# Attention scores of sixteen small heads: sixteen tiles of 32 by 32 of the array in place of four of 32 by 128

## The chip, the core and the metric

The kernel runs on one core of a Trainium2 chip. A core has five engines that run at the same time and wait for one another through semaphores: TensorE (PE, matrix products), VectorE (DVE), ScalarE (ACT), GpSimd (POOL) and SyncE (SP, which here only issues DMAs). PE reads both operands from SBUF and writes its results to PSUM. A PE product takes two kinds of instruction: a weight load puts the stationary operand into the array (the profile calls this row PEld), and a matmul then streams the moving operand through it (row PE). All data here are f32, and one product of the program becomes two weight loads and two matmuls in the profile; this text calls such a load and matmul together a pass, so a product has two passes. (A transpose through PE has one.)

The metric is device time in microseconds (us) of one execution. Lower is better.

## The reference

Sixteen independent sequences of 256 positions with 256 channels go through two blocks. Every attention has 16 heads of 16 channels.

- Block 0: adaptive layer norm from `cond`; self-attention in windows of 128 positions (shifted by 64); adaptive layer norm; cross-attention to a context of 256 positions that keeps only the 16 largest scores of each row; adaptive layer norm; a gated feed-forward with 1024 hidden channels. Each part is added to the residual through a gate.
- Block 1: adaptive layer norm of the sequence and of the context, full cross-attention of 256 queries to 256 keys, projection, residual.

Cut to the lines that the change touches, the scores are

```python
scores = jnp.einsum('bnqhd,bnkhd->bnhqk', q, k) / jnp.sqrt(jnp.float32(D))   # block 0, windows of 128
scores = jnp.einsum('bqhd,bkhd->bhqk', q, k) / jnp.sqrt(jnp.float32(D))      # block 0, top 16 of 256 keys
top_s, top_i = jax.lax.top_k(scores, TOPK)
scores = jnp.einsum('bqhd,bkhd->bhqk', q, k) / jnp.sqrt(jnp.float32(dh))     # block 1, 256 keys
```

with D = dh = 16: every score is a sum over only 16 products.

## The kernel before, in words

The whole program is unrolled: 16 sequences, one after another, overlapped like a pipeline. The helpers record operations (`op`) with an engine, a cost, the buffers that they read and write and a due time from a table (`DUE`, written out by hand for every operation). `Plan.order` sorts all operations by due time; each engine then executes its own operations in exactly that order. Nothing is reordered at run time between operations of one engine, so an operation that waits holds up everything behind it on its engine. Costs and due times only shape the order when the program is built.

PSUM has eight banks, each 128 partitions by 512 f32 values (buffers `W`). A score operation takes four of them at once.

How the scores are laid out: queries and keys are channel-major, 128 channels (8 heads) in the partitions. A strip of 32 partitions holds two heads of 16 channels; the keys `k2` exist twice, each copy with the other head's channels replaced (`by_parity`), so a product over 32 partitions gives the scores of one head. The helper `four` (L681) records one PE operation that does the four strips of 32 partitions: strip j uses rows 32j to 32j+31 of the array and writes its own bank j. Such a product uses 32 rows and 128 columns of the array; the four strips lie in different rows, so that they can run at the same time. This text calls one such operation a score group. There are five kinds, named by their line before the change:

- L948, `topk_round`: 128 queries against 256 keys for two heads: one product of 512 columns in each strip.
- L1067, `last_attention`, first half: scores of which only the row maxima are taken (`maxima`, DVE): two products of 256 columns in each strip.
- L1079, `last_attention`, second half: the scores again, transposed (keys in the partitions), for the exponentials on ACT: two products of 256 columns in each strip (four of 128 in the last sequence, which is done in two tiles).
- L901, `self_attention`, first half, for the row maxima: four products of 128 columns in each strip.
- L909, `self_attention`, second half, transposed: four products of 128 columns in each strip (two in sequence 15).

Between the two halves, `lower` (L710) turns the row maxima on DVE (L716) and writes them with eight small DMAs on SP's queue for each half of the heads (L723) into unused rows of the queries `q2`, so that the second half's product subtracts them by itself. Each of these DMAs writes one block of 32 columns (`k` in its loop) in every group of 128 of `q2`. It has to wait until the first half's products have read what it overwrites, and the second half's products wait for it.

After the exponentials, `weighted` (L699) multiplies them with the values. It is a PE operation of another shape: 128 rows and 17 columns of the array, four products side by side in four different groups of 32 columns (`po.t[ds(NW * j, DH + 1), ...]`). Before a score group, and after it, PE usually does other products of 128 by 128.

The stationary operand of a score product, which is loaded as weights, is a block of 128 queries (L948, L1067, L901) or 128 keys (L1079, L909), `ts(k, P)` in the code; the moving operand is the other one.

## Time and profile before

| | us |
|---|---|
| median of 3 runs | 1333.25 (1332.62 to 1334.47) |
| the profiled execution | 1333.42 |
| its span, first to last instruction | 1331.6 |
| PE busy | 1317.7 (99%), 13476 matmuls and as many weight loads |
| DVE busy | 1201.9 (90%) |
| ACT busy | 1019.5 (77%) |
| POOL busy | 1019.4 (77%) |

The profiled execution took 1.8 us more than its span, for what lies before the first and after the last instruction. Matmuls are pipelined and their ends are modelled, so that PE's busy share says little by itself; the chain of work that ended last says more. In it, each piece is given with its start, the time until the next piece, the line and the number of instructions.

The instructions of the five score lines in the profile: 512 matmuls of L948, 1024 of L1067, 960 + 128 of L1079, 1024 of L901 and 1024 of L909, 4672 in all, each with a weight load of 128 columns.

### The profile page before, as it was taken

The numbers are of one execution on the slowest core, as the hardware profiler recorded it, in microseconds if no ns is written. First come the engines' busy times: TensorE is split into PE (matmuls) and PEld (weight loads), VectorE is DVE, ScalarE is ACT, GpSimd is POOL, SyncE is SP. The second block draws the span as 40 slices with busy tenths as digits, with TensorE's granted clock in tenths as the row PEclk, the third lists the DMA queues.
The fourth block names the chain that finished last, engine by engine and source line by source line (L and its number), as shares of the span: only waits on it lengthen the run. The fifth ranks groups of instructions, "written<-read, shape, count | busy, mean of one in ns | idle before, by whom it ended". The sixth has DMA issues, their size and how long they took to land.

```text
span 1331.6 us, 38422 instructions
## 1 busy us (share of the span) xinstructions
PE 1317.7 (99%) x13476; PEld 1029.3 (77%) x13476; DVE 1201.9 (90%) x4298; ACT 1019.5 (77%) x2359; POOL 1019.4 (77%) x1522
## 2 busy tenths in 40 slices
PE   8999999999999999999999999999999999999998
PEld 6778887777878787787878777787878777786885
DVE  5698988999999999999999999999999999999844
ACT  3698878778787777878777877868777786977774
POOL 3587886868878786887869687887978688878862
PEclk9999999999999999999999999999999999999999
DMA  5454122102011110201111110101111020100000
GB/s 182 156 194 169 43 81 66 50 10 65 3 27 50 33 50 19 57 8 36 35 26 50 26 50 10 49 19 27 49 26 50 12 57 2 48 20 11 16 2 18
DMA packets 71647, 63.31 MB, mean 48 GB/s; under 512 B 38595, under 2 KB 57583, under 8 KB 71199
## 3 DMA queue, kind: packets, MB, share of 16 engines
q1 hardware_dynamic: 71455, 60.86, 15.6%
q8 instruction: 107, 1.75, 0.5%
q14 instruction: 85, 0.70, 0.2%
HBM read 45.58 MB, written 14.73 MB: 45 GB/s over the span
## 4 chain that ended last, share of the span: by engine, by line
PE 83%; DVE 12%; POOL 1%; DMA 1%; SPq 1%; issue 1%; ACT 0%; POOLq 0%; DVEq 0%; ACTq 0%
PE W L1009 18%; PE W L594 10%; PE W L699 9%; PE W L1036 8%; PE W L644 7%; PE W L1079 6%; PE W L948 5%; PE W L677 5%; PE W L630 4%; DVE nm L706 3%; DVE rest L975 3%; PE W L909 3%; DVE top L967 2%; PE W L901 2%; PE W L568 2%; PE W L1067 2%
## 5 line engine op out<-in xcount | busy, mean ns | idle before, releaser
L996 POOL TENSOR_TENSOR prT<-rest,prT 128x512 f32<-128x512 f32 x256 | 324.2, 1274 | 101.5 <-DVE rest L992 97.2
L706 DVE TENSOR_REDUCE nm<-W 128x2 f32<-128x512 f32 (+1 forms) x384 | 238.0, 678 | 22.3 <-PE W L1067 15.1
L1009 PE MATMUL W<-xT,w_L_xcond_w_m 128*128 128x256 f32 (+1 forms) x1088 | 257.4, 374 | 0.2 <-ACT xT L582 0.2
L980 ACT ACTIVATE prT<-W,ntop 128x256 f32<-128x256 f32 x512 | 214.4, 501 | 43.8 <-POOL ntop L969 38.0
L730 ACT ACTIVATE pTO<-W 128x512 f32<-128x512 f32 (+1 forms) x392 | 205.4, 611 | 33.1 <-PE W L1079 27.8
L1009 PEld LDWEIGHTS W<-xT,w_L_xcond_w_m 128*128 128x128 f32 x1088 | 185.0, 190 | 53.6 <-ACT pTO L730 10.6
L975 DVE MATCH_REPLACE8 rest<-top,W 128x256 f32<-128x256 f32 x512 | 207.4, 415 | 0.0
L967 DVE MAX8 top<-W 128x8 f32<-128x256 f32 x512 | 184.9, 415 | 24.1 <-PE W L948 24.1
L992 DVE MATCH_REPLACE8 rest<-top,rest 128x256 f32<-128x256 f32 x512 | 204.8, 409 | 0.0
L987 DVE MAX8 top<-rest 128x8 f32<-128x256 f32 x512 | 186.8, 409 | 0.0
L647 ACT ACTIVATE pTT<-W 128x512 f32<-128x512 f32 x256 | 152.2, 617 | 2.8 <-PE W L644 2.5
L644 PE MATMUL W<-ident,prT 128*128 128x128 f32 x1024 | 140.2, 274 | 0.2 <-POOL prT L996 0.2
L644 PEld LDWEIGHTS W<-ident,prT 128*128 128x128 f32 x1024 | 120.4, 141 | 17.5 <-POOL prT L996 0.4
L1036 PE MATMUL W<-w_L_xcond_w_m,h 128*128 128x256 f32 x512 | 113.8, 380 | 0.0
L1026 POOL TENSOR_TENSOR mb<-ma,mb 128x256 f32<-128x256 f32 (+1 forms) x136 | 95.1, 700 | 24.3 <-ACT mb L1024 21.6
L1036 PEld LDWEIGHTS W<-w_L_xcond_w_m,h 128*128 128x128 f32 x512 | 97.0, 190 | 14.5 <-POOL h L1029 1.1
L660 POOL TENSOR_TENSOR on<-tr,rec 128x256 f32<-128x256 f32 (+1 forms) x132 | 65.2, 503 | 49.4 <-DVE rec L659 49.3
L1029 POOL TENSOR_TENSOR h<-h,mb 128x256 f32<-128x256 f32 (+1 forms) x136 | 94.8, 697 | 8.7
L699 PE MATMUL W<-pTO,v 128*17 128x128 f32 (+1 forms) x2112 | 99.2, 323 | 0.0
L657 DVE STREAM_TRANSPOSE tr<-W 128x512 f32<-128x512 f32 (+1 forms) x132 | 72.6, 552 | 27.0 <-PE W L699 17.0
L1024 ACT ACTIVATE mb<-W,half 128x256 f32<-128x256 f32 (+1 forms) x136 | 68.7, 506 | 34.8 <-PE W L1009 34.0
L1019 ACT ACTIVATE h<-W,half 128x256 f32<-128x256 f32 (+1 forms) x136 | 68.7, 505 | 24.3 <-PE W L1009 24.2
(129 smaller groups left out, 2653.9 us busy)
## 6 DMA issues: line engine op xcount, KB each, us to landing
gate<-gates SPq DMA_DIRECT2D x48, 256.0 KB
q<-nmT SPq DMA_DIRECT2D x480, 1.0 KB
kept_k<-k SPq DMA_DIRECT2D x13, 512.0 KB
k<-kept_k SPq DMA_DIRECT2D x13, 512.0 KB
cx<-in_ctx_dram SPq DMA_DIRECT2D x19, 256.0 KB
kept_v<-v SPq DMA_DIRECT2D x13, 272.0 KB
v<-kept_v SPq DMA_DIRECT2D x13, 272.0 KB
cx<-in_ctx_dram SPq DMA_DIRECT2D x104, 32.0 KB
```

What stands on the lines that cost most here:

```text
L644: nc.tensor.transpose(w.t[:, ts(n, P)], flat[:, ts(n, P)], ident)
L699: nc.tensor.matmul(po.t[ds(NW * j, DH + 1), ds(q0, nq)], v.t[:, kt, 8 * m + 2 * j + a, :], pT.t.rearrange("p n q -> p (n q)")[:, ds(part, ...
L706: op("DVE", 0.61, lambda j=j, s=s: nc.vector.tensor_reduce(nm.t[:, k, ds(j, groups, step=4)], s.t.rearrange("p (g k) -> p g k", g=groups), ...
L730: op("ACT", 0.24 + q * 0.0005, lambda s=s, pT=pT: nc.scalar.activation(pT.t.rearrange("p n q -> p (n q)")[:, :q], s.t[:, :q], AF.Exp), r=[ ...
L967: nc.vector.max(top.t[:, a, 0:8], s.t[:, ts(a, L)])
L975: nc.vector.match_replace(rest.t[:, a, :], top.t[:, a, 0:8], s.t[:, ts(a, L)], TAKEN)
L980: nc.scalar.activation(pr.t[:, a, :], s.t[:, ts(a, L)], AF.Exp, bias=ntop.t[:, a:a + 1])
L987: nc.vector.max(top.t[:, a, 8:16], rest.t[:, a, :])
L992: nc.vector.match_replace(rest.t[:, a, :], top.t[:, a, 8:16], rest.t[:, a, :], TAKEN)
L996: op("POOL", 1.25, lambda: nc.gpsimd.tensor_tensor(pr.t, rest.t, pr.t, ALU.mult), r=[rest, pr], w=[pr])
L1009: nc.tensor.matmul(w.t[:, :q], w_m1.t[:, c, ds(n0, P)], xT.t[:, c, :q], start=c == 0, stop=c == NCC - 1)
L1036: nc.tensor.matmul(pp.t[:, ts(k, C)], hs[f].t[:, ts(k, P)], w_m2.t[:, f, :], start=f == 0, stop=f == NHC - 1)
```

## The change

Every score product is cut into four: the stationary operand's 128 columns are loaded as four blocks of 32 (`NW` = 32), each with a product of its own that writes 32 of the bank's 128 partitions. So a product uses 32 rows and 32 columns of the array, and a score group addresses sixteen such tiles in place of four. The moving operand, the results, the banks, the costs given to the planner, the due times and with them the order of all operations stay as they are. Within a group, the loop goes over the pieces, then over the four column blocks `c`, then over the four strips `j`.

```diff
         def all_of_them():
             for piece in pieces:
-                for j, s in zip(groups, banks):
-                    emit(slice(32 * j, 32 * j + 32), s.t, *piece)
+                for c in range(P // NW):
+                    for j, s in zip(groups, banks):
+                        emit(slice(32 * j, 32 * j + 32), s.t[ts(c, NW)], NW * c, *piece)
...
-                            lambda rows, s, n, m, a, k=k: nc.tensor.matmul(
-                                s[:, ts(n, P)], q2.t[rows, m, a, ts(k, P)], k2.t[rows, m, a, ts(k, P)], start=True, stop=True),
+                            lambda rows, s, at, n, m, a, k=k: nc.tensor.matmul(
+                                s[:, ts(n, P)], q2.t[rows, m, a, ds(k * P + at, NW)], k2.t[rows, m, a, ts(k, P)], start=True, stop=True),
...
-        banks, made = four([()], lambda rows, s: nc.tensor.matmul(
-            s, q.t[rows, m, ts(k, P)], k2.t[rows, m, :, :], start=True, stop=True),
+        banks, made = four([()], lambda rows, s, at: nc.tensor.matmul(
+            s, q.t[rows, m, ds(k * P + at, NW)], k2.t[rows, m, :, :], start=True, stop=True),
```

The other three calls of `four` (L909, L1067 and L1079) change in the same way: the stationary operand's `ts(k, P)` or `ts(kt, P)` becomes a block of 32 columns that starts at `at`. One line is added ahead of these calls, so the lines after L686 are numbered one higher after the change.

In the built program the score products grow from 2336 to 9344. With two passes each, PE has 27492 matmuls and 27492 weight loads in place of 13476 of each. The other engines' work is the same, instruction for instruction, but the semaphore waits change: which block of `q2` each small DMA of `lower` has to wait for is now known by blocks of 32 columns, so that 529 waits of their own stand in front of these DMAs on SP in place of 155. DVE gets 109 more waits of their own (509 in place of 400), most of them in front of the maxima of the top-16 search (L967) and the row maxima (L706).

More of the change, by code (lines that the diff above doesn't have):

```diff
@@ L908, in self_attention @@
             banks, _ = four([(nt * a + k, a, k) for a in range(2) for k in range(nt)],
-                            lambda rows, s, n, a, k, m=m: nc.tensor.matmul(
-                                s[:, ts(n, P)], k2.t[rows, m, a, ts(k, P)], q2.t[rows, m, a, ts(k, P)], start=True, stop=True),
+                            lambda rows, s, at, n, a, k, m=m: nc.tensor.matmul(
+                                s[:, ts(n, P)], k2.t[rows, m, a, ds(k * P + at, NW)], q2.t[rows, m, a, ts(k, P)], start=True, stop=True),
                             0.45 * nt, [(q2, m), (k2, m)], pTs)
@@ L1066, in last_attention @@
             for k in range(nt):
-                banks, _ = four([(a,) for a in range(2)], lambda rows, s, a, k=k, m=m: nc.tensor.matmul(
-                    s[:, ts(a, L)], q2.t[rows, m, a, ts(k, P)], k2.t[rows, m, a, :], start=True, stop=True),
+                banks, _ = four([(a,) for a in range(2)], lambda rows, s, at, a, k=k, m=m: nc.tensor.matmul(
+                    s[:, ts(a, L)], q2.t[rows, m, a, ds(k * P + at, NW)], k2.t[rows, m, a, :], start=True, stop=True),
                     0.87, [(q2, m), (k2, m)], [nm])
@@ L1078, in last_attention @@
                 banks, _ = four([(NT * e + kt, a, kt) for e, a in enumerate(pair) for kt in range(NT)],
-                                lambda rows, s, n, a, kt, m=m: nc.tensor.matmul(
-                                    s[:, ts(n, q)], k2.t[rows, m, a, ts(kt, P)], q2.t[rows, m, a, :q], start=True, stop=True),
+                                lambda rows, s, at, n, a, kt, m=m: nc.tensor.matmul(
+                                    s[:, ts(n, q)], k2.t[rows, m, a, ds(kt * P + at, NW)], q2.t[rows, m, a, :q], start=True, stop=True),
                                 0.87, [(q2, m), (k2, m)], pTs)
```

## The prediction

> **What bounds the kernel now.** I read the page first: the busy shares, the granted clock, the chain that ended last; then PE's waits, then the chain in order of time, then single stretches of a few hundredths of a us.

> ```profile
> span 1331.6 us, 38422 instructions
> PE 1317.7 (99%) x13476; PEld 1029.3 (77%) x13476; DVE 1201.9 (90%) x4298; ACT 1019.5 (77%) x2359; POOL 1019.4 (77%) x1522
> PEclk9999999999999999999999999999999999999999
> PE 83%; DVE 12%; POOL 1%; DMA 1%; SPq 1%; issue 1%; ACT 0%; POOLq 0%; DVEq 0%; ACTq 0%
> ```

> PE is busy all the time, at the full granted clock, and it carries 83% of the chain. Its waits, longest first, add up to a few us:

> ```profile
> PE W L807 <- DVE h L802: 3.7, 1, 3.7
> PE W L594 <- ACT xT L582: 1.1, 2, 0.5
> PE W L781 <- DMA h<-in_L_xcond_b_ada_dram: 0.9, 1, 0.9
> PE W L677 <- DVE oT L667: 0.8, 3, 0.3
> PE W L909 <- DMA q<-nmT: 0.6, 1, 0.6
> ```

> So whatever a score group becomes longer or shorter by goes one to one into the time, as long as nothing else comes late. The chain in order of time (start, time to the next piece, line, instructions) gives what a group takes:

> ```profile
> 613.90 1.10 PE W L901 x32
> 615.01 0.99 PE W L699 x16
> 616.00 1.07 PE W L1079 x16
> ...
> 619.43 1.07 PE W L948 x8
> ```

> The reader is to compare L1079 with L699: 16 matmuls each, 256 columns each, four tiles side by side each. L699 is 0.08 us shorter. Their weights differ: 128 columns in L1079, 17 in L699, and the loads of 17 columns are shorter by about the same:

> ```profile
> L699 PEld LDWEIGHTS W<-pTT,v 128*17 128x17 f32 x2048 | 53.3, 97 | 20.8 <-ACT pTT L647 14.0 <-issue 1.7 <-ACT prT L980 0.8
> L948 PEld LDWEIGHTS W<-k,q 32*128 32x128 f32 x512 | 20.1, 183 | 17.6 <-ACT pTO L730 6.1 <-issue 5.7 <-DVE rest L992 3.3
> ```

> So only a group's first load is exposed, later ones lie under running matmuls. Last, how tiles start; for stretches of one L948 group (length, then busy time and instructions of PE and PEld so far), and after them of the L699 group behind it:

> ```profile
> 619.36:619.37 0.01, 0.01 (x1) 0.01 (x1) 1.00 0.00 0
> 619.36:619.38 0.02, 0.01 (x3) 0.02 (x3) 1.00 0.00 0
> 619.36:619.39 0.03, 0.03 (x4) 0.03 (x4) 1.00 0.00 0
> 619.36:619.50 0.14, 0.14 (x4) 0.14 (x8) 1.00 0.00 0
> 619.36:619.92 0.56, 0.56 (x8) 0.31 (x8) 1.00 0.01 2
> ...
> 620.43:620.60 0.17, 0.16 (x4) 0.13 (x8) 1.00 0.00 0
> 620.43:620.70 0.27, 0.26 (x8) 0.17 (x12) 1.00 0.00 0
> ```

> Four first passes start within 0.03 us (the trace's stamps are 619.365, .372, .378 and .385: 6.7 ns apart), then all second weights load, and the second passes start only after 0.53 us. A group ends when the tile that started last has streamed all its columns. The columns that a tile streams are not changed: no tile becomes faster for having fewer weights.

> **The change part by part.** Groups: 512/8 of L948, 1024/16 of L1067, 960/16 + 128/32 of L1079, 1024/32 of L901 and 960/32 + 64/16 of L909 make 64 + 64 + 64 + 32 + 34 = 258.

> (1) The exposed load becomes shorter. 17 columns take 97 ns, 128 take 183; at 32 a straight line between them gives 97 + 15/111 x 86 = 109, so 74 ns less for each group: 258 x 0.074 = -19.1 us. Bounds: -0.086 (all that L699 has over L948) to 0 for each group.

> (2) Sixteen tiles start one after another in place of four: 12 more starts of 6.7 ns are 80 ns for the last tile: 258 x 0.080 = +20.6 us. Bounds: 0 if tiles of different column blocks start together; 12 x 10 ns, the coarsest spacing that the three stretches allow, 0.12 for each group, +31.0. I take 6.7 because L699's four tiles, which differ in columns, and L948's, which differ in rows, both start so. Together (1) and (2) come to +1.5 us: almost nothing, but a difference of two terms of 20.

> [...]

> (3) The 66 groups of 128 columns have no slack. L901 takes 1.10 us for 8 rounds of four matmuls; without some 0.2 for first load and drain a round is 0.112 us. Now 16 passes must start in each round: 16 x 6.7 ns = 0.107. It fits, barely. Lower bound 0; upper bound, if starts space out to 8 ns, 0.128 a round, 0.13 for each group, +8.6 us. I take a quarter, 0.03: +2.0 us.

> (4) SP's queue. 374 more waits stand in front of the small DMAs of L723, that is 5.5 in each chain of eight (68 chains). Such a wait costs 28 ns in the median row, and 0.07 us with the gap around it, by the pace of single DMAs in the trace: 0.15 to 0.39 us for a chain, double for the second chain of self-attention. Who waits: the second-half products (L909, L1079), and behind them all of PE. Typically this is covered: the chain below ends at 377.16 and its L1079 group starts at 379.66; in the one case where PE waited, PE went on 1.7 us after the last DMA's issue began, so here some 1.3 us are spare.

> ```profile
> 372.48 4.68 SPq L723 DMA_DIRECT2D q<-nmT  x8
> ```

> By the starts of the groups behind them, about a dozen of the 68 have less than 0.5 us to spare; at 0.2 us each +2.4 us. Bounds: 0 (all hidden), 12 x 0.39 = +4.7.

> (5) DVE's 109 more waits at 21 ns (the median row of such waits in front of L967 and L706) are 2.3 us on an engine that has 130 us idle; those in front of L967 delay the freeing of banks. Half is taken, +1.0; bounds 0 and +2.3. POOL and ACT: nothing moves there; their idle time of 23% covers what comes some ns later. Instruction fetch: the instruction queue q8 moved 1.75 MB at 0.5% of the DMA engines; twice that is still 1%, taken as nothing. If a fetch came late, PE itself would stall: it would use 256 instructions (16 KB) in one L901 group of 1.1 us, where now it uses them in some 12 us.

> The sum: 1.5 + 2.0 + 2.4 + 1.0 = +6.9 us on the profiled execution's 1333.42 us, which is 0.2 above the median: 1340.

> [...]

> **Rivals.** *Faster.* The stagger of the starts hides better than the loads' saving: if a further tile costs less than 6.2 ns, (1) outweighs (2). For it: a queue with all sixteen products ready has four times the choice. Against it: the four starts are as far apart in the groups whose data was long ready. At 4.5 ns: 258 x (0.054 - 0.074) = -5.2; with (3) to (5) covered 1328. The end, no stagger at all, is 1314.

> *Nothing.* (1) and (2) cancel and (3) to (5) stay under cover: 1334.9. For it: both prices come from the same rows, and PE waited for such a DMA once. Within 0.2% (2.7 us, about what a measurement of this kernel can tell from no change) means 10 ns for each group, so this case is narrow.

> *Much slower.* PE cannot hold sixteen tiles of two passes. Where only 12 run at a time, a group's 0.85 us of streaming becomes a third longer: 258 x 0.28 = +73, 1407. Where passes cannot be fed faster than in the densest lasting row (L699, 32 passes in 0.99 - 0.10 us, 28 ns a pass), L948 stays, L1067 and L1079 need 64 x 0.028 = 1.78 and 66 groups of 128 passes 3.56: 128 x 0.89 + 66 x 2.67 = +290, 1624. Against it: passes start 6.7 ns apart in bursts, and the compiled program has the two passes of a product next to each other, yet in the stretches four first passes start ahead of any second one, so PE does pick ahead in its queue.

> **How the numbers follow.** Slightly slower, +2.7 to +45 us: 0.48, forecast 1340. Faster: 0.22. Nothing: 0.16. Much slower: 0.14. The range leaves out the much slower case (0.14) and the far end of the faster one (0.04): 1322 to 1385; the likeliest alone has 1336 to 1360. Slower by over 0.2%: 0.48 + 0.14 = 0.62; within: 0.16; faster: 0.22.

> **What would show it.** (1): first and second pass of a tile 0.08 us closer than before. (2): stretches at a group's start with 16 matmuls within 0.11 us; L948 x32 in the chain at 1.06 to 1.09. (3): L902 and L910 (x128) at 1.10 to 1.20, above the others' change. (4): PE waits for q<-nmT of more than 0.6 us. (5): DVE's waits for L949. The prediction is wrong if PE's spacing of starts is not 6.7 ns across rows and columns at once, or if groups of sixteen leave gaps between rounds.

## The result and the profile after

| | before | after |
|---|---|---|
| median (lowest to highest), us | 1332.93 (1331.89 to 1334.47) | 1453.82 (1450.32 to 1455.64) |
| span of the profiled execution, us | 1331.6 | 1451.2 |

The ratio is 1.0903, with a 95% interval of 1.0879 to 1.0927. The forecast was 1340 with a range of 1322 to 1385, so the change costs some 120 us where 7 were expected, and lies outside the range. These are the lines of the page after that answer to those shown of before (line numbers after L686 are one higher):

```profile
span 1451.2 us, 66938 instructions
PE 1423.3 (98%) x27492; PEld 1079.4 (74%) x27492; DVE 1204.7 (83%) x4298; ACT 1024.3 (71%) x2359; POOL 1020.9 (70%) x1522
PEclk9999999999999999999999999999999999999999
q8 instruction: 216, 3.54, 1.0%
PE 95%; issue 1%; DMA 1%; ACT 1%; DVE 1%; POOL 1%; SPq 0%; POOLq 0%; ACTq 0%; DVEq 0%
```

PE is still the bound (95% of the chain) and its granted clock is unchanged (nine tenths or more in every slice, as before). What grew is mostly the time that PE calls busy (1317.7 to 1423.3 us), and that lies in the score groups. The chain in order of time (start, us to the next piece, line, instructions) shows it:

```profile
663.39 1.42 PE W L1080 x62
...
668.90 1.99 PE W L902 x98
670.89 0.99 PE W L700 x16
...
675.66 1.07 PE W L949 x32
...
681.41 1.86 PE W L910 x103
```

L949 takes 1.07 us as before, although it too runs in sixteen tiles. L1080 went from 1.07 to 1.42, L902 from 1.10 to 1.99. The three differ in the number of products in a group: 16 of 512 columns, 32 of 256, 64 of 128. All stream the same number of columns. (The number of instructions in a chain piece can fall short of a group's.)

Summed over the execution, from the first start of each group to the first start of the next work on PE (worked out from the trace's start stamps, waits included; in 12 places PE starts a product of L902 while the last ones of an L1080 group still start, and the table counts from there, which moves some 5 us from L1080 to L902):

| line (after) | products in a group | before, us | after, us | change |
|---|---|---|---|---|
| L949 | 16 | 68.3 | 70.0 | +1.6 |
| L1068 | 32 | 71.2 | 95.4 | +24.2 |
| L1080 | 32, one of 64 | 77.1 | 98.3 | +21.2 |
| L902 | 64 | 35.4 | 78.8 | +43.4 |
| L910 | 64, some of 32 | 36.9 | 63.3 | +26.3 |

That is 116.7 of the 119.6 us that the span grew. Those 12 early starts also correct the description of the kernel before: PE does begin an operation ahead of the end of the one before it. That the other engines keep strictly to their order is not shown here.

Among PE's waits (us in total, times, longest) those on issue are new, and the one for the small DMAs is gone. A single wait of 2.0 us for a weight is new too; it also stands in the kernels below that are as fast as before, with 1.2 to 2.4 us:

```profile
PE W L902 <- issue: 9.5, 7, 3.1
PE W L808 <- DVE h L803: 3.7, 1, 3.7
PE W L1080 <- issue: 3.5, 9, 0.7
PE W L594 <- DMA w_L_xcond_w_qkv<-in_L_xcond_w_qkv_dram: 2.0, 1, 2.0
...
PE W L910 <- issue: 0.5, 2, 0.3
```

So some 13.5 us are waits for nothing that the profile shows, and about 103 us are inside the groups. Stretches from the start of one group show where. Columns: stretch, length, busy time and instructions of PE and of PEld, granted clock, DMA share, GB/s. First an L949 group, then an L1080 group, then an L902 group, each with only its own line's instructions:

```profile
675.59:675.70 0.11, 0.10 (x16) 0.11 (x28) 1.00 0.06 8
675.59:676.03 0.44, 0.43 (x16) 0.23 (x32) 1.00 0.02 2
675.59:676.15 0.56, 0.56 (x32) 0.23 (x32) 1.00 0.01 2
...
663.31:663.43 0.12, 0.11 (x15) 0.11 (x28) 1.00 0.58 176
663.31:663.67 0.36, 0.35 (x31) 0.35 (x33) 1.00 0.68 190
663.31:663.95 0.64, 0.63 (x33) 0.45 (x34) 1.00 0.74 190
663.31:664.10 0.79, 0.78 (x42) 0.59 (x50) 1.00 0.70 182
663.31:664.46 1.15, 1.14 (x64) 0.82 (x64) 1.00 0.77 176
...
668.83:669.25 0.42, 0.42 (x33) 0.34 (x34) 1.00 0.07 20
668.83:669.54 0.71, 0.71 (x46) 0.59 (x51) 1.00 0.04 12
668.83:670.39 1.56, 1.56 (x112) 1.44 (x117) 1.00 0.02 5
```

In L949 sixteen matmuls start within 0.11 us, all 32 weights are loaded by 0.44 us, and the second passes start together. In L1080 the first 32 passes go just as well: 31 matmuls have started by 0.36 us. Then there is nothing to start: at 0.64 us there are 33 matmuls and 34 loads, though the first tile has streamed its product by 0.45 us and the last by 0.57, and by that they are free (an estimate: 27 ns of load and 427 of stream; where these come from stands in the last section). After 0.65 us matmuls start again, but the first passes of the next products come only every 16.7 ns (stamps 0.649, 0.666, 0.683, 0.699 us from the first matmul, and so on). In L902 the same stop comes after 33 passes, and behind it passes come one in 14 ns on average ((112 - 33) in 1.56 - 0.42 us). That gave the theories to be tried.

### The profile page after: what moved, and what is told of

The parts are those of the page before. It is cut to its first block, busy times and chain, and to the rows that moved or that the text cites. A ratio compares the mean times of both kernels' runs of the same rounds, so it can differ in the third digit from the quotient of the medians.

```text
span 1451.2 us, 66938 instructions
## 1 busy us (share of the span) xinstructions
PE 1423.3 (98%) x27492; PEld 1079.4 (74%) x27492; DVE 1204.7 (83%) x4298; ACT 1024.3 (71%) x2359; POOL 1020.9 (70%) x1522
## 3 DMA queue, kind: packets, MB, share of 16 engines
q8 instruction: 216, 3.54, 1.0%
## 4 chain that ended last, share of the span: by engine, by line
PE 95%; issue 1%; DMA 1%; ACT 1%; DVE 1%; POOL 1%; SPq 0%; POOLq 0%; ACTq 0%; DVEq 0%
PE W L1010 16%; PE W L594 11%; PE W L700 11%; PE W L644 8%; PE W L1037 8%; PE W L1080 7%; PE W L1068 6%; PE W L677 6%; PE W L630 6%; PE W L949 5%; PE W L910 4%; PE W L902 4%; PE W L568 3%; PE W L825 1%; DMA w_L_xcond_w_qkv<-in_L_xcond_w_qkv_dram 1%
## 5 line engine op out<-in xcount | busy, mean ns | idle before, releaser
L1010 PE MATMUL W<-xT,w_L_xcond_w_m 128*128 128x256 f32 (+1 forms) x1088 | 257.4, 374 | 0.2 <-ACT xT L582 0.2
L1010 PEld LDWEIGHTS W<-xT,w_L_xcond_w_m 128*128 128x128 f32 x1088 | 185.0, 190 | 58.5 <-ACT pTO L731 11.7
L968 DVE MAX8 top<-W 128x8 f32<-128x256 f32 x512 | 184.8, 414 | 41.5 <-PE W L949 36.1
L647 ACT ACTIVATE pTT<-W 128x512 f32<-128x512 f32 x256 | 151.3, 613 | 4.1 <-PE W L644 4.0
L1080 PE MATMUL W<-q,k 32*32 32x256 f32 (+1 forms) x4352 | 106.1, 373 | 4.4 <-issue 3.5
L700 PE MATMUL W<-pTO,v 128*17 128x128 f32 (+1 forms) x2112 | 100.3, 323 | 0.1
L1068 PE MATMUL W<-k,q 32*32 32x256 f32 x4096 | 98.8, 385 | 0.0
```

What stands on the lines that cost most here:

```text
L700: nc.tensor.matmul(po.t[ds(NW * j, DH + 1), ds(q0, nq)], v.t[:, kt, 8 * m + 2 * j + a, :], pT.t.rearrange("p n q -> p (n q)")[:, ds(part, ...
L1010: nc.tensor.matmul(w.t[:, :q], w_m1.t[:, c, ds(n0, P)], xT.t[:, c, :q], start=c == 0, stop=c == NCC - 1)
L1080: lambda rows, s, at, n, a, kt, m=m: nc.tensor.matmul(s[:, ts(n, q)], k2.t[rows, m, a, ds(kt * P + at, NW)], q2.t[rows, m, a, :q], start=T ...
```

## The experiments

Four theories stood against each other. A, B and D were written down ahead of the first four kernels below; C was put into these words after them, and ahead of all others.

- **Queue (C).** PE holds at most 16 products ahead, 64 instructions, in program order. A place comes free only when the oldest product is through, about 190 ns after its stream has ended, and places are refilled at one product per 16.7 ns. These are estimates from the L1080 group above: some 32 passes (16 products of two loads and two matmuls) before the stop, a restart at 0.649 us where the oldest product's stream ends at some 0.454, and the stamps behind it.
- **Feed (A).** A stock of about 32 passes, and behind it one pass per 13 to 17 ns, whatever has finished; the figures are from the same stretches of L1080 and L902.
- **Loads (B).** A supposition: that a load into rows in which a matmul runs is not hidden. It is priced at 27 ns for 32 columns, an estimate from the first and the second pass of a tile in L949, 533 ns apart before and 453 after: 80 ns for 96 columns.
- **Instructions (D).** Four times the score instructions have to be fetched, and that is what costs.

### One kind of group at a time

The helper `four` gets a width for each call. In the first three kernels one kind of score group keeps the sixteen tiles (`nw=32`: L949; L1068 and L1080; L902 and L910) and the others go back to four; the fourth has eight tiles of 32 by 64 (`nw=64`) for L949, L1068 and L1080, and four for self-attention.

```diff
-    def four(pieces, emit, cost, r, also=(), after=(), groups=range(4)):
+    def four(pieces, emit, cost, r, also=(), after=(), groups=range(4), nw=P):
...
-                for c in range(P // NW):
+                for c in range(P // nw):
                     for j, s in zip(groups, banks):
-                        emit(slice(32 * j, 32 * j + 32), s.t[ts(c, NW)], NW * c, *piece)
+                        emit(slice(32 * j, 32 * j + 32), s.t[ts(c, nw)], nw * c, *piece)
...
```

> Only the top-16 groups (L948) in sixteen tiles, all others in four. Theory A (PE starts about 32 passes of a group 6.7 ns apart, and is fed one pass per 13 to 17 ns after that): these groups have 32 passes, so they stay at 1.07 us, and the time at 1333, within 3 us. Theory B (a load into rows in which a matmul runs is not hidden, 27 ns each): 8 loads in a row group are 216 ns in place of 107, 64 groups, +7 us: 1340. Theory D (the cost goes with the number of added instructions, by their fetch): 1536 of the 14016 added passes, 11% of the 120 us, +13: 1346.

> Only the last attention's groups (L1067, L1079) in sixteen tiles. A: 64 passes a group, +24.2 and +21.2 us by the start-to-start sums of the changed kernel: 1378. B: 16 loads of 27 ns in a row group in place of 107 exposed, +0.325 us for each of 128 groups, +42: 1375. D: 6336 of 14016 added passes, 45% of 120, +54: 1387.

> Only the self-attention's groups (L901, L909) in sixteen tiles. A: 128 passes in almost every group, +43.4 and +26.4 us by the start-to-start sums: 1403. B: 32 loads of 27 ns in a row group are 0.86 us, +0.76 for each of 66 groups, +50: 1383. D: 6144 of 14016 added passes, 44% of 120, +53: 1386.

> Eight tiles of 32 by 64 for L948, L1067 and L1079; self-attention in four as before. A: no group has more than 32 passes, so nothing is slowed; the first load of 64 columns takes 53 ns in place of 107, four more starts cost 27: -27 ns for each of 192 groups, -5 us: 1328. B: in a row group twice the loads of half the length, no change: 1333. D: 2624 added passes, 19% of 120, +22: 1355.

| sixteen tiles for | median, us | ratio to before (95%) | A | B | D |
|---|---|---|---|---|---|
| L949 only | 1334.53 | 1.0007 (0.9998 to 1.0017) | 1333 | 1340 | 1346 |
| L1068 and L1080 only | 1386.09 | 1.0388 (1.0374 to 1.0402) | 1378 | 1375 | 1387 |
| L902 and L910 only | 1389.41 | 1.0416 (1.0400 to 1.0432) | 1403 | 1383 | 1386 |
| none; eight tiles for L949, L1068, L1080 | 1332.66 | 0.9993 (0.9985 to 1.0002) | 1328 | 1333 | 1355 |

C has no figures on record for these four. B falls with the first row: the second weights of all sixteen tiles load into rows in which matmuls run (in the stretch above all 32 loads are done by 0.44 us, ahead of the second passes), and the group stays at 1.07 us. D as the whole cause falls with the first and the last row, where the added instructions should have cost 13 and 22 us. But D's numbers fit the two middle rows, where A is 8 too low and 14 too high. The third row shows part of why: L902's sum is 65.3 us here and 78.8 in the changed kernel, with the same code on that line. Of these 13.5 us some 6 are waits on issue (9.5 us there, 3.8 here), and some 5 are the early starts of L902 that the table above takes from L1080, whose sum is 104 us in the second row's kernel and 98.3 in the changed one. The sum of the three changes, 1.2 + 52.8 + 56.1 = 110 of 121 us, leaves about 11 to their meeting.

The fourth row settles less. Each L949 group took 1.044 us and each L1080 group 1.049, 27 ns less, just as the exposed load (53 in place of 107 ns) and four more starts say. But where two L1068 groups follow each other they took 2.17 us in place of 2.14, and the total gained 0.7 us of the 5 expected, not to be told from nothing. B's 1333 fits this row as well.

### The number of products alone, and their order

Now only L949 has sixteen tiles, and its products are cut into two halves of 256 columns. Nothing else changes: the same columns, no new wait, no neighbour. In the second kernel the two halves of a tile follow each other in program order.

```diff
-        banks, made = four([()], lambda rows, s, at: nc.tensor.matmul(
-            s, q.t[rows, m, ds(k * P + at, 32)], k2.t[rows, m, :, :], start=True, stop=True),
+        banks, made = four([(0,), (1,)], lambda rows, s, at, a: nc.tensor.matmul(
+            s[:, ts(a, L)], q.t[rows, m, ds(k * P + at, 32)], k2.t[rows, m, a, :], start=True, stop=True),
...
```
```diff
...
+            if nw == 32:
+                for c in range(P // nw):
+                    for j, s in zip(groups, banks):
+                        for piece in pieces:
+                            emit(slice(32 * j, 32 * j + 32), s.t[ts(c, nw)], nw * c, *piece)
+                return
...
```

> Top-16 groups in sixteen tiles, each product of 512 columns cut into two of 256: 32 products (64 passes) a group, the same columns streamed. Theory C (PE holds at most 16 products, 64 instructions, in program order; the places come free only when the oldest product is through, some 190 ns after its stream, and are then refilled at one product per 16.7 ns): 27 + 427 + 190 + 15 x 16.7 + 427 + 85 ns, about 1.41 us in place of 1.07, +22 us: 1355. Theory A (a stock of 32 passes, behind it one pass per 16.7 ns whatever has ended): the last product is there at 0.65 us, a group 1.15: 1338.

> As with the two halves of 256 columns, but the two halves of one tile follow each other in program order (c, then j, then the halves). C: the first 16 products are now only eight tiles; the other eight get in when the oldest products are through, the second of them at 27 + 854 + 190 = 1071 ns, the last tile at about 1.3 us, and stream 0.85: about 2.25 us a group, +75 us: 1408. A: the last tile's first pass is there at 0.58 us, a group 1.5 us: 1362.

Measured: 1356.52 us (ratio 1.0166, 1.0150 to 1.0182) and 1407.79 us (1.0555, 1.0540 to 1.0570), where C said 1355 and 1408 and A said 1338 and 1362. The chains in order of time, first of the halves, then of the halves in the other order (where L949 is L955):

```profile
647.71 1.42 PE W L949 x60
```
```profile
445.82 2.29 PE W L955 x64
```

By the start stamps all 64 groups take 1.424 us in the one and 2.254 in the other, within 2 ns. The first could have been read off L1080 beforehand, since C's numbers were taken from there; the second could not. The tiles, the columns and the number of instructions are the same in both, only the order in the program differs, and the group is 0.83 us longer. So the inference is that what limits is not a rate but what fits into the queue in program order: with the halves adjacent, the first 16 products are only eight tiles. The stamps show it: in the second kernel eight first passes start within 0.1 us, 13.3 ns apart, the 33rd matmul starts at 0.86 us, as the first tile's two halves end, and only from 1.08 us do products come in again, where C's text has 1.071.

### A group without small tiles

The kernel before, in which the 60 groups of L699 that stream 256 columns (in the last attention) are cut into products of 32 columns: 64 products in place of 8, in four tiles of 128 by 17.

```diff
-            for a, kt, part, q0, nq, first, last in pieces:
-                for j, pT in enumerate(pTs):
+            wide = pieces[0][4] == 256
+            for b0 in range(0, 256, 32) if wide else (0,):
+                for a, kt, part, q0, nq, first, last in pieces:
+                    for j, pT in enumerate(pTs):
+                        w = 32 if wide else nq
+                        nc.tensor.matmul(po.t[ds(NW * j, DH + 1), ds(q0 + b0, w)], v.t[:, kt, 8 * m + 2 * j + a, :],
+                                         pT.t.rearrange("p n q -> p (n q)")[:, ds(part + b0, w)], start=first, stop=last)
```

> No small tiles at all: before, with the 60 groups of L699 that stream 256 columns (in L1084's call) cut into products of 32 columns: 128 passes in four tiles of 128 by 17, the same columns streamed, 0.99 us a group before. C: 16 products last 213 ns, the oldest is through at 14 + 53 + 190 = 257 ns, then one product per 16.7 ns where 13.3 would be needed: 257 + 48 x 16.7 + 85 = 1.15 us, +0.16 for 60 groups, +10 us: 1343. A: (128 - 32) x 16.7 + 0.1 = 1.7 us, +43: 1376. A third cost, loads of 14 ns one after another over all four tiles, would make 128 x 14 = 1.8 us, +49: 1382.

Measured: 1384.65 us (1.0377, 1.0359 to 1.0394). The total hits the third cost, but that is an accident, as the groups show. Of 44 groups that stand alone, 23 take between 1.24 and 1.29 us, the others 1.5 to 2.7. L703, which is L699 here, takes 43 us more than before: 60 undisturbed groups would make 15 of them, the waits on issue below 9.8, and where the rest comes from is not shown. In a group of 1.24 us all 128 loads lie within 1.05 us, 8 ns each, so that they don't take turns at 14 ns (17 columns at 0.83 ns); and from the 33rd pass on products start every 17 ns (827 ns for 48). That is C's pace, in tiles of full height; A's 1.7 us is not the undisturbed time. C's 1.15 us was 0.09 too short. Most of the longer groups stand still at one place, some of them long enough to be counted as waits:

```profile
PE W L703 <- issue: 9.8, 12, 2.6
PE W L811 <- DVE h L806: 3.8, 1, 3.8
PE W L1083 <- issue: 2.6, 3, 1.1
```

These are the waits of L902 in the changed kernel again, and here too they come where many short instructions follow each other.

### The supply of instructions

L902 in sixteen tiles, each group issued three times over (the same scores are written again).

```diff
-            for piece in pieces:
+            for piece in (list(pieces) * 3 if nw == 32 else pieces):
```

> Self-attention in sixteen tiles (the others in four), and each group of L901 issues its four pieces three times over, which writes the same scores again: 3 x 256 instructions in a row for 32 groups. C alone: 1.85 us for each repetition, as a group takes with no wait, 64 x 1.85 = +118 on the 1389 of the version with self-attention alone: 1508. If the supply of instructions (queue q8, blocks of 16 KB that start at least 3.3 us apart in every run so far, 256 instructions each) is a bound of its own: up to 3.3 us for each repetition, +211: 1600, with PE's waits on issue grown to some 90 us.

That text counts L910 in sixteen tiles, but in this kernel it is in four. So both expectations are 26 us too high: 1482 for C alone, 1574 with the supply as a bound. Measured: 1604.82 us (1.2036, 1.2017 to 1.2054), 31 above the second: about half of that because a repetition took 3.54 us in place of 3.3, half in rows outside the repeated groups (L700 +7, L1080 +5, L630 +3, L594 +2). PE's waits and a part of the chain:

```profile
PE W L902 <- issue: 107.8, 64, 4.6
```
```profile
669.74 3.40 PE W L902 x185
673.15 1.21 issue
674.36 2.01 PE W L902 x104
676.37 1.46 issue
677.83 0.44 PE W L902 x12
```

L902's sum is 292.0 us against 65.3 with single groups: 226.7 / 64 = 3.54 us for each repetition of 256 instructions, of which (107.8 - 3.8) / 64 = 1.6 are the wait on issue (3.8 us of it stood there with single groups) and 1.9 the group. The queue q8 moves blocks of 16 KB, and one block holds some 255 PE instructions (216 packets for 54984 matmuls and loads in the changed kernel, 107 for 26952 in the one before, whose page has the line below). By their stamps two blocks never started closer than 3.25 us in any kernel here; it was 3.33 in the changed kernel and 3.32 in this one, and 5.65 in the kernel before.

```profile
q8 instruction: 107, 1.75, 0.5%
```

The stamps also tie the waits to the blocks one by one: all 64 waits of L902 here end 2.3 to 2.9 us after a block on q8 has started, and all 18 waits on issue of score groups in the changed kernel end 2.2 to 2.8 us after one, though only 13% of all its matmuls start 2.2 to 3.0 us after a block. So the supply of instructions is taken as a second bound, and the waits on issue as its mark.

### What is left to gain

L949 and L1080 in eight tiles of 32 by 64 (`nw=64`), L1068 and self-attention in four; and the same with self-attention in eight.

> Eight tiles of 32 by 64 for L948 and L1079 only; L1067, whose groups often follow each other, and self-attention in four. C: 16 products a group, all within the queue: -27 ns for each of 64 + 58 groups, -3.3 us: 1330. Theory that the saving of 27 ns is lost elsewhere, as most of it was with L1067 in eight tiles too: 1332 to 1333.

> As the version with L948 and L1079 in eight tiles of 32 by 64, and self-attention (L901, L909: four products of 128 columns in each strip) in eight as well: 32 products, 64 passes a group. C: the oldest product is through at 53 + 213 + 190 = 456 ns, and a tile needs its third product only at 480, so nearly nothing is late; the last tile ends near 1.0 + 0.085 us, 1.09 in place of 1.10 for 62 groups, -1 us on the 1331.6 of that version: 1331. A (what counts is the number of passes: 64, as in a group of L1080 that takes 1.42): +0.32 for each, +20: 1352.

The first: 1331.62 us, ratio 0.9981 (0.9972 to 0.9990), 2.3 us below the kernel before by the medians, where C had 3.3 and the other theory 1 to 2; it does not decide between them. The chain has the group at 1.05 us:

```profile
674.00 1.05 PE W L1080 x32
```

The second: 1337.42 us, 1.0027 (1.0015 to 1.0038). L910 takes 1.14 us in most groups; L902 takes 1.24 behind products of L1010 and 1.12 behind L1080. C had 1.09 and A 1.42. So 64 passes do not cost what A says, but C was too kind: in an L910 group the third products of tiles 5 to 8 start 16.7 ns apart in place of 6.7, and each round adds to that. Why L902 loses more behind L1010 (in the kernel with self-attention alone too: 1.99 us in place of 1.83) stays open.

## Why the prediction was wrong

**(1), the exposed load: right.** 74 ns were taken. A tile's second pass starts 450 to 455 ns after its first in L949, 453 in most, where it was 533: 80 ns. The 109 and 183 ns of the working are not what is exposed (that is 27 and 107 ns); only their difference carries over, and the profile after has 103 ns for 32 columns, so 80.

**(2), the stagger: right.** Sixteen tiles start 6.7 ns apart, across rows and columns alike: 100 ns from first to last in 37 of the 64 groups of L949, and 117 to 121 in 22 others, nearly all of them behind L700. With (1) the sum had +6 ns for each group. L949 as a whole grew by 1.6 us for 64 groups, 25 ns for each, and the kernel with L949 alone in sixteen tiles is at most 2.3 us slower than the one before.

**(3), the groups of short products: this is the step that failed.** It had +2.0 us for 66 groups of 128 columns, because 16 starts of 6.7 ns fit into a round, and nothing for the 128 groups of 256 columns. Measured: +69.7 us (L902, L910) and +45.4 (L1068, L1080), with 10.0 and 3.5 of waits on issue in them. The 6.7 ns are the spacing of a group's first sixteen products; behind the stop those of L1080 come 16.7 ns apart, and the step took the first for a pace that PE can hold. A group of 32 or 64 products does not fit into C's 16 places. From C's terms an L1080 group is 27 + 427 + 190 ns until the oldest product's place is free, 15 x 16.7 for the refill, 427 for the last product and some 90 until the next group (what L949's 1.07 us leave after 100 of starts, 453 and 427): 1.41 us, measured 1.42. (The 190 and the 16.7 were read from such groups, so this sum is no test; the one with the order of the halves is.) The same terms for a group of 64 products, 27 + 4 x 213 + 3 x 190 + 15 x 16.7 + 90 ns, make an estimate of 1.79 us, where L902 took 1.83 and more and L910 1.86 and more: most of it, not all. The prediction's own sign of being wrong, gaps between the rounds of sixteen, is what came. The prediction saw that PE picks ahead, and its sum did not ask how far. Nor did PE keep to program order: with the halves adjacent, the first passes of eight tiles started within 0.1 us, ahead of the first tile's second half at 0.43 us, which stands second in the program.

**(4), SP's waits: not seen.** +2.4 us were taken; PE's waits after have no line for q<-nmT. The work ahead of them became slower, so the term was not tested.

**(5), DVE and the instruction fetch.** DVE's waits for the top-16 scores grew from 24.1 to 36.1 us, but PE makes 95% of the chain, so that this is taken as a consequence; no run separates the +1.0 us that was taken. The fetch was taken as nothing by its share of the DMA engines, 1%. This is the second step that failed. The share was right (1.0%) and the wrong measure: what counts is how close one block follows another (3.33 us at the closest). The waits on issue are 13.5 us, and all 18 of them end 2.2 to 2.8 us after a block has started; the sentence that PE would stall if a fetch came late was the right one.

**The rivals.** "Much slower" had the right idea, that PE cannot hold sixteen tiles of two passes, but both its prices were off. 12 tiles at a time would have hit L949 too, which stayed at 1.07 us. 28 ns a pass came from L699, a row that is limited by streaming and not by the feed (an estimate: each of its four tiles streams 8 x 128 columns, at 427 ns for 512 that is 0.85 of the 0.99 us); L1080 shows 1.42 / 64 = 22 ns and L902 1.99 / 128 = 16. "Faster" and "nothing" would have been decided by (1) and (2), which did cancel.

## What to carry to other kernels

Before work is cut into more and smaller pieces, count the instructions of everything that must run side by side, in program order: here, with the halves adjacent, the tiles beyond the first 64 instructions got no product until 1.08 us, and the group took 2.25 us in place of 1.42. A spacing of starts that is read from a burst is no rate; look for a group in the trace that is longer than the burst, or say that there is none. And a queue's share of the DMA engines said nothing here on whether one instruction block follows another in time: it was 1.0%, with 13.5 us of waits on issue. 256 short PE instructions, repetition after repetition, took 3.54 us each on average, 1.6 of them waits on issue.
